# Attention: a batch's layer norm turned by VectorE in blocks of 32 by 32 and sorted by memory, one turn ahead, in place of TensorE transposes

## The chip, the cores and the metric

The kernel runs on one core of a Trainium2 chip. A core has five engines that work side by side, each through its own list of instructions in order: TensorE (PE in the profile; PEld is its weight load), VectorE (DVE), ScalarE (ACT), GpSimd (POOL) and SyncE (SP, which here issues nearly all DMAs). Sixteen DMA engines move data between memory and the core's on-chip memory of 128 partitions (rows); TensorE writes its results to eight banks called PSUM. The metric is the device time of one execution in microseconds.

## What is computed

Three residual blocks over x of 16 batches, 512 tokens and width 256, all in 32-bit floats: half of a feed-forward block (attention over 16 slots and 16 experts), full causal attention with 16 heads, and half of the same feed-forward block again. The change is in the middle one:

```python
x = x + 0.5 * _L0_ffn_ref(_layernorm(x, axis=-1), ...)
x = x + _L0_attn_ref(_layernorm(x, axis=-1), ...)
x = x + 0.5 * _L0_ffn_ref(_layernorm(x, axis=-1), ...)

# _L0_attn_ref: q, k rotated; causal
q = x @ Wq + bq;  kv = x @ Wkv + bkv
scores = jnp.einsum('bqhd,bkhd->bhqk', q, k) * (1.0 / np.sqrt(DQK))
probs = jax.nn.softmax(jnp.where(causal, scores, -jnp.inf), axis=-1)
out = jnp.einsum('bhqk,bkhd->bqhd', probs, v)
return out.transpose(0, 2, 1, 3).reshape(b, s, H * DV) @ Wo + bo
```

The products with Wq and Wk need the layer norm with the width on the partitions, while the layer norm is made with tokens on the partitions. So each batch's layer norm has to be transposed, 512 x 256.

## The kernel before

All of x stays on chip: 16 places `xs[b]`, tokens on the partitions, 4 tiles of 128 tokens by 256.

**Units and turns.** Attention works on 64 units: 16 batches (`b`) times 4 groups (`hg`) of 4 heads. The loop `for u in range(-2, nu)` (L1101) is a pipeline, and one pass of it is called a turn here. Turn u does, for different units: the products of the weights with the values of unit u (`sums`, p_av), the turning of the weights of unit u+1 (`turn_most`, `turn_corner`, `turn_rest`, `move`), scores and exponentials of unit u+2 (p_as), queries and keys of unit u+3 (`queries_keys`, p_q and p_k), values of unit u+1 (p_v), and the output product of unit u (`leave`, p_ay), whose addition to x by VectorE (`added`, kept in `gone`) follows in the next turn.

**Order.** TensorE's order is that of the program throughout. Inside the loop so is that of VectorE, ScalarE, GpSimd and SyncE (`manual_schedule`, L1098). So an instruction waits for all that stand ahead of it on its engine. TensorE's order in a turn: p_av, (p_ahT), p_as of tile 3, p_v, p_q, p_k, p_v, p_as of tiles 2, 1 and 0, p_ay.

**A new batch.** In turn u = 4b + 1 the batch b + 1 comes in (`fresh`, L1105). `enter` (L866) makes its layer norm h on ScalarE from mean and deviation, in two tiles that share their places with two of the rotation's (`rope2`, `rope3`). `with_bias` (L874) adds the output's bias to x on GpSimd. `width` (L878) turns h: 8 TensorE transposes of 128 by 128 into two banks of PSUM (p_ahT, L883), and two ScalarE copies (L884) into `ahT`, of which there are two. In the same turn p_q reads `ahT`. Batch 0 enters before the loop.

**Deviations.** The statistics of tokens (`token_stats`) run ahead by `u + 13`; a pair of batches has its square root on ScalarE (`spread`) in turn u with u + 5 a multiple of 8, and its reciprocal on VectorE (`scales`) one turn later. ScalarE loads another table for the square root and then the one for the exponential again.

**The turning of the weights.** VectorE transposes only within blocks of 32 by 32 (L1001, `STREAM_TRANSPOSE`, into `sq`); 16 DMAs (`move`, L1024, 160 KB each) carry the blocks to their partitions in `prT`, from on-chip memory to on-chip memory. `sq` and `prT` have one buffer each. The slot stage of the feed-forward block does the same through memory: `Squares.turn` (L530), `leave` (L534, one DMA of 512 KB to memory) and `onto` (L538, four DMAs back).

**SyncE** in a turn: the 16 DMAs of `move`, and, in the turn after a batch's last unit (u = 4b), two writes of the result (L1078). The DMAs use eight semaphores in rotation, so a DMA also waits for the one issued eight before it.

Of the kernel before, what the change touches and what calls it, by code (L numbers as in the profile page):

```python
# [9 lines left out]
F32 = mybir.dt.float32  # L10
# [5 lines left out]
P = 128  # L16
NB, S, D = 16, 512, 256
NT = S // P
NC = D // P
GB = 4  # L20
PB = 2
# [14 lines left out]
NHG = AH // HG  # L36
SQ = 32
NSQ = P // SQ
# [9 lines left out]
def macaron_kernel(ctx: ExitStack, tc: tile.TileContext, a: dict, out: bass.AP):  # L48
    nc = tc.nc
# [6 lines left out]
    def ps(name):  # L56
        return psum.tile([P, 512], F32, tag="b", name=name, bufs=8)
# [135 lines left out]
    def token_stats(b, t):  # L193
        g = b // PB
        if b % PB == 0 and t == 0:
            mvs[g] = small.tile([P, PB * NT, 2], F32, tag=f"mv{g}", name=f"mv{g}", bufs=2)
        st = small.tile([P, 6], F32, tag="bnst", name=f"bnst{b}_{t}")
        nc.vector.bn_stats(st, xs[b][:, t, :])
        nc.vector.bn_aggr(mvs[g][:, (b % PB) * NT + t, :], st)
# [17 lines left out]
    def pair_shift(g):  # L217
        shifts[g] = small.tile([P, PB * NT], F32, tag="shift", name=f"shift{g}", bufs=2)
        nc.vector.scalar_tensor_tensor(shifts[g], mvs[g][:, :, 0], -1.0, rstds[g], ALU.mult, ALU.mult)
# [624 lines left out]
    def attention(qp, wq, wk, wv, wo, cos, sin, row):  # L844
# [2 lines left out]
        ap = None  # L847
        units = [(b, hg) for b in range(NB) for hg in range(NHG)]
        nu = len(units)
        hTs, hs, qs, ks, vs, oTs, prTs, stds = {}, {}, {}, {}, {}, {}, {}, {}  # L850

        def spread(g):

            n = PB * NT
            std = small.tile([P, n], F32, tag="std8", name=f"std_g{g}")
            nc.scalar.activation(std, mvs[g][:, :, 1], AF.Sqrt, bias=eps)
            return std

        def scales(g, std):

            n = PB * NT
            rstds[g] = small.tile([P, n], F32, tag=f"rstd{g}", name=f"rstd{g}", bufs=1)
            nc.vector.reciprocal(rstds[g], std)
            pair_shift(g)

        def enter(b):  # L866

            hs[b] = [qp.tile([P, 2, D], F32, tag=f"rope{2 + k}", name=f"h{b}_{k}") for k in range(2)]
            for t in range(NT):
                i = (b % PB) * NT + t  # L870
                nc.scalar.activation(hs[b][t // 2][:, t % 2, :], xs[b][:, t, :], AF.Identity,
                                     bias=shifts[b // PB][:, i:i + 1], scale=rstds[b // PB][:, i:i + 1])

        def with_bias(b):  # L874
            for t in range(NT):
                nc.gpsimd.tensor_tensor(xs[b][:, t, :], xs[b][:, t, :], row, ALU.add)

        def width(b):  # L878
            hTs[b] = qp.tile([P, NC, S], F32, tag="hT", name=f"ahT{b}", bufs=2)
            for c in range(NC):  # L880
                pt = ps(f"p_ahT{b}_{c}")
                for t in range(NT):
                    nc.tensor.transpose(pt[:, t * P:(t + 1) * P], hs[b][t // 2][:, t % 2, c * P:(c + 1) * P], ident)  # L883
                nc.scalar.copy(hTs[b][:, c, :], pt)  # L884

        class Rotated:

# [2 lines left out]
            def __init__(self, u, nm, w, r):  # L890
                self.b, self.hg = units[u]
                self.nm, self.w, self.r, self.m = nm, w, r, {}
# [172 lines left out]
        def leave(u, t0):  # L1065
            b, hg = units[u]
            py = ps(f"p_ay{b}_{hg}_{t0}")
            for t in range(2):
                for pair in range(HG // 2):
                    nc.tensor.matmul(py[:, t * D:(t + 1) * D], oTs[u][:, pair, (t0 + t) * P:(t0 + t + 1) * P],  # L1070
                                     wo[:, hg * (HG // 2) + pair, :],
                                     start=(pair == 0), stop=(pair == HG // 2 - 1))

            def added():
                xt = xs[b][:, t0:t0 + 2, :]
                nc.vector.tensor_tensor(xt, py.rearrange("p (t d) -> p t d", t=2), xt, ALU.add)
                if hg == NHG - 1:
                    nc.sync.dma_start(xout[b][:, t0:t0 + 2, :], xt)  # L1078
            return added
# [4 lines left out]
        def queries_keys(u):  # L1084

            if u >= nu:
                return []
            q = qs[u] = Rotated(u, "q", wq, R_BQ)
            k = ks[u] = Rotated(u, "k", wk, R_BK)
            return [lambda: q.half(0), lambda: (q.half(1), q.add()), lambda: k.half(0), lambda: (k.half(1), k.add())]  # L1090

        scales(0, spread(0))
        enter(0)
        with_bias(0)
        ap = yield [lambda: width(0)] + queries_keys(0)
        ws = {}
        seen = 2 * NHG
        with tc.manual_schedule(engines={mybir.EngineType.DVE, mybir.EngineType.Activation,  # L1098
                                         mybir.EngineType.Pool, mybir.EngineType.SP}):
            gone = []  # L1100
            for u in range(-2, nu):  # L1101
                new = ws[u + 2] = Weights(u + 2) if u + 2 < nu else None
                qk = queries_keys(u + 3)
                old = ws.get(u + 1)
                fresh = u + 3 < nu and units[u + 3][1] == 0  # L1105
                if fresh:
                    enter(units[u + 3][0])
                if u + 2 == nu:
                    old.scaled((1, 0))
                    values(u + 1, 0)  # L1110
                    values(u + 1, 2)
                if u >= 0:
                    sums(u, 0)
                    sums(u, 1)
                if old and u + 2 == nu:
                    old.turn_at_once()
                elif old:
                    old.turn_most(0)
                    old.scaled((1, 0), slice(0, HG // 2))
                    old.turn_most(1)  # L1120
                    old.scaled((1, 0), slice(HG // 2, HG))
                    old.turn_most(2)
                    old.turn_most(3)
                    old.turn_corner()
                    old.turn_rest()
                    old.move()
                for one in gone:
                    one()
                if fresh:
                    with_bias(units[u + 3][0])  # L1130
                if u + 4 in stds:
                    scales((u + 4) // (PB * NHG), stds.pop(u + 4))
                if fresh:
                    width(units[u + 3][0])
                if new:
                    new.scores((3,))
                    new.exps((3,))

                for at in range(seen, min(u + 13, NB * NHG)):
                    token_stats(*divmod(at, NHG))  # L1140
                seen = max(seen, u + 13)
                if u >= NHG + 1:
                    token_stats(*divmod(u - NHG - 1, NHG))
                if new:
                    new.scaled((3,))
                if 0 <= u + 1 < nu - 1:
                    values(u + 1, 0)
                for one in qk:
                    one()
                if 0 <= u + 1 < nu - 1:  # L1150
                    values(u + 1, 2)
                if 0 <= u + 5 < nu and (u + 5) % (PB * NHG) == 0:
                    stds[u + 5] = spread((u + 5) // (PB * NHG))
                if new:
                    new.scores((2,))
                    new.scores((1, 0))
                    new.exps((2,))
                    new.exps((1, 0), lambda: new.scaled((2,)))

                if u == nu - NHG:  # L1160
                    for g in range(NB // PB - 1):
                        pair_rstd(g)
                if u == nu - 1:
                    for g in range(PB):
                        entered[g] = xs[g]
                        for t in range(NT):
                            i = (g % PB) * NT + t
                            nc.vector.tensor_scalar(xs[g][:, t, :], xs[g][:, t, :], mvs[g // PB][:, i, 0:1],
                                                    rstds[g // PB][:, i:i + 1], ALU.subtract, ALU.mult)
                gone = [leave(u, 0), leave(u, 2)] if u >= 0 else []  # L1170
                if u >= nu - 2:
                    for one in gone:
                        one()
                    gone = []
            token_stats(NB - 2, NT - 1)
# [55 lines left out]
```

## Time and profile before

| | us |
|---|---|
| median of 3 runs | 2330.49 (2329.22 to 2330.73) |
| profiled execution, its own time | 2332.58 |
| its span, first to last instruction | 2330.9 |
| mean granted clock of TensorE | 0.993 |

| groups that the change touches (count) | busy us | mean ns of one |
|---|---|---|
| L883 PE MATMUL p_ahT 128x128 (128) | 17.4 | 279 |
| L884 ACT COPY ahT 128x512 (32) | 17.0 | 585 |
| L871 ACT ACTIVATE h 128x256 (64) | 33.1 | 588 |
| L876 POOL TENSOR_TENSOR x 128x256 (64) | 44.7 | 730 |
| L1001 DVE STREAM_TRANSPOSE sq 128x512 (126) | 84.3 | 669 |
| L530 DVE STREAM_TRANSPOSE sqa 128x512 (50) | 34.7 | 708 |
| L898 PE MATMUL p_q 128x512 (512) | 230.5 | 593 |

Durations of TensorE overlap, since matmuls are pipelined: what a group takes is read from the start of it to the start of the next. A line of a timeline has start, length, engine, line, operation, what is written and read, and a count; the time in brackets is idle time before it and what ended it. A line of the table by stretch has, for PE, PEld, DVE, ACT and POOL, busy us and instructions, then TensorE's granted clock, the share of the DMA engines and their GB/s. SyncE's lines stand as SPq: it only issues.

### The profile page before, as it was taken

How to read it: one execution, taken by the hardware profiler on the slowest of the kernel's cores; microseconds unless marked ns; L12 is line 12 of the kernel's file. 1: busy time of each engine (PE TensorE's matmuls, PEld its weight loads, DVE VectorE, ACT ScalarE, POOL GpSimd, SP SyncE). 2: the span in 40 equal slices, each digit the busy share in tenths (PEclk: the TensorE clock that was granted, in tenths of full speed). 3: DMA queues.
4: the chain of work that ended last, by engine and by line, in shares of the span. 5: the costliest groups of instructions: out<-in, count | busy, mean ns of one | idle time of the engine just before them, and what ended most of it. 6: DMA issues, size and time to landing. Idle time of an engine off the chain costs nothing. (4 is left out here: it accounts for less than half of the span.)

```text
span 2330.9 us, 42260 instructions
## 1 busy us (share of the span) xinstructions
PE 2285.0 (98%) x14496; PEld 1453.5 (62%) x14496; DVE 1754.1 (75%) x4658; ACT 1123.7 (48%) x3046; POOL 1061.9 (46%) x1692
## 2 busy tenths in 40 slices
PE   7999999999999999999999999999999999999999
PEld 5665588465656565565656565655656566664588
DVE  6742397888888888898888888888888874442387
ACT  4743243455455545554645545554555454542233
POOL 2210054565555565655656555556565541210043
PEclk9999999999999999999999999999999999999999
DMA  6839851345555464645455555546464543839834
GB/s 223 252 124 406 321 137 46 85 97 129 107 119 126 103 134 93 142 103 129 107 123 113 126 111 116 129 100 137 91 140 105 127 110 96 241 115 405 329 115 140
DMA packets 159710, 346.77 MB, mean 149 GB/s; under 512 B 38980, under 2 KB 98952, under 8 KB 151304
## 3 DMA queue, kind: packets, MB, share of 16 engines
q1 hardware_dynamic: 158636, 343.27, 55.4%
q8 instruction: 115, 1.88, 0.4%
q14 instruction: 99, 0.81, 0.1%
q10 hardware_dynamic: 860, 0.81, 0.1%
HBM read 148.95 MB, written 29.88 MB: 77 GB/s over the span
## 5 line engine op out<-in xcount | busy, mean ns | idle before, releaser
L986 POOL TENSOR_SCALAR pr<-pr,ars 128x512 f32<-128x512 f32 (+3 forms) x1024 | 522.1, 532 | 631.5 <-DVE ars L983 631.5
L978 ACT ACTIVATE pr<-pr,amn 128x512 f32<-128x512 f32 (+3 forms) x1024 | 560.5, 549 | 268.4 <-DVE amn L974 268.2
L974 DVE CUSTOM_DVE_ANT_0 pr<-p_as,causal 128x512 f32<-128x512 f32 (+3 forms) x1024 | 433.9, 484 | 96.6 <-PE p_as L956 96.6
L1001 DVE STREAM_TRANSPOSE sq<-pr 128x768 f32<-128x768 f32 x441 | 379.0, 906 | 0.2 <-issue 0.2
L956 PE MATMUL p_as<-k,q 32*128 32x128 f32 (+3 forms) x4096 | 325.3, 445 | 7.1 <-DVE k L904 3.4
L1054 PE MATMUL p_av<-prT,v 128*64 128x512 f32 (+3 forms) x2048 | 292.1, 438 | 1.9 <-DVE amn L974 1.9
L956 PEld LDWEIGHTS p_as<-k,q 32*128 32x128 f32 x4096 | 192.4, 186 | 107.4 <-issue 49.6
L920 PEld LDWEIGHTS p_v<-wv,ahT 128*128 128x128 f32 x1024 | 189.4, 190 | 97.4 <-issue 75.6
L920 PE MATMUL p_v<-wv,ahT 128*128 128x256 f32 x1024 | 248.1, 385 | 0.0
L923 ACT COPY v<-p_v 128x512 f32<-128x512 f32 x128 | 73.3, 574 | 353.1 <-PE p_v L920 353.1
L1070 PE MATMUL p_ay<-wo,aoT 128*128 128x256 f32 x1024 | 240.5, 388 | 0.2 <-ACT aoT L1061 0.2
L1054 PEld LDWEIGHTS p_av<-prT,v 128*64 128x64 f32 x2048 | 138.1, 138 | 161.7 <-issue 136.5
L898 PE MATMUL p_k<-ahT,wk 128*128 128x512 f32 x512 | 230.6, 592 | 0.4 <-DVE amn L974 0.4
L898 PE MATMUL p_q<-ahT,wq 128*128 128x512 f32 x512 | 230.5, 593 | 0.2 <-ACT ahT L884 0.2
L1070 PEld LDWEIGHTS p_ay<-wo,aoT 128*128 128x128 f32 x1024 | 190.8, 191 | 32.0 <-ACT aoT L1061 0.6
L978 ACT ACTIVATION_READ_ACCUMULATOR pr<-pr,amn 128x1 f32 x1024 | 191.7, 187 | 0.0
L898 PEld LDWEIGHTS p_k<-ahT,wk 128*128 128x128 f32 x512 | 97.2, 190 | 122.7 <-issue 110.5
L898 PEld LDWEIGHTS p_q<-ahT,wq 128*128 128x128 f32 x512 | 97.1, 190 | 95.8 <-issue 85.4
L717 POOL TENSOR_TENSOR kbd<-kT,own 128x256 f32<-128x256 f32 x32 | 19.7, 619 | 267.4 <-DVE kT L680 235.5
L1061 ACT ACTIVATE aoT<-p_av,bcol 128x512 f32<-128x512 f32 x128 | 87.4, 684 | 108.9 <-PE p_av L1054 108.9
L770 PE MATMUL p_cy<-vw,catT 128*128 128x256 f32 x512 | 120.8, 379 | 0.0
L548 PE MATMUL p_ds<-hT,qk 128*128 128x512 f32 x256 | 118.3, 606 | 2.3 <-ACT hT L241 2.3
(167 smaller groups left out, 3252.0 us busy)
## 6 DMA issues: line engine op xcount, KB each, us to landing
prT<-sq SPq DMA_DIRECT2D x1008, 160.0 KB
w<-in_e_W_dram SPq DMA_DIRECT2D x64, 1024.0 KB
w<-in_e_Wg_dram SPq DMA_DIRECT2D x32, 1024.0 KB
out_dram<-x SPq DMA_DIRECT2D x64, 256.0 KB
awaya<-sqa SPq DMA_DIRECT2D x25, 512.0 KB
atT<-awaya SPq DMA_DIRECT2D x100, 128.0 KB
xl<-in_attn_x_dram SPq DMA_DIRECT2D x16, 512.0 KB
xl<-out_dram SPq DMA_DIRECT2D x16, 512.0 KB
```

The source lines that it names most:

```text
L548: nc.tensor.matmul(psc, qk[:, k, c * P:(c + 1) * P], hT[:, k, :], start=(k == 0), stop=(k == NC - 1))
L770: nc.tensor.matmul(py[:, t * D:(t + 1) * D], atT[:, c, t * P:(t + 1) * P], vws[b][:, c, :], start=(c == 0), stop=(c == NC - 1))
L898: nc.tensor.matmul(pq, self.w[:, k, at:at + P], hTs[self.b][:, k, :], start=(k == 0), stop=(k == NC - 1))
L920: nc.tensor.matmul(pv[:, t * 256:(t + 1) * 256], hTs[b][:, k, (t0 + t) * P:(t0 + t + 1) * P], wv[:, k, hg * HG * DQ:(hg + 1) * HG * DQ], s ...
L956: nc.tensor.matmul(banks[j][:, at:at + w], q[n][j * 32:(j + 1) * 32, i * P:(i + 1) * P], k[n][j * 32:(j + 1) * 32, :w], start=(n == 0), st ...
L974: nc.vector.tensor_tensor_reduce(out=self.at(i, j), in0=banks[j][:, at:at + w], in1=causal[:, S - w:], scale=-1.0 / math.sqrt(DQ), scalar= ...
L978: nc.scalar.activation(self.at(i, j), self.at(i, j), AF.Exp, bias=self.mn[:, i, j:j + 1], scale=-1.0, accum_out=self.rs[:, i, j:j + 1])
L986: nc.gpsimd.tensor_scalar(self.at(i, j), self.at(i, j), self.rs[:, i, j:j + 1], 1.0, ALU.mult, ALU.mult)
L1001: nc.vector.transpose(view(self.sq, j * blocks * SQ + dst[0] * SQ, [(blocks * SQ, nh)] + [(s * SQ, n) for s, (_, n) in zip(dst[1:], of)] + ...
L1054: nc.tensor.matmul(po[j * DQ:(j + 1) * DQ, :].rearrange("d (a f) -> d a f", a=NSQ)[:, :, t * SQ:], vs[u][:, t, head * DQ:(head + 1) * DQ], ...
L1061: nc.scalar.activation(oTs[u][:, pair, :].rearrange("d (i a y) -> d a i y", i=NT, a=NSQ), po.rearrange("d (a i y) -> d a i y", i=NT, a=NSQ ...
L1070: nc.tensor.matmul(py[:, t * D:(t + 1) * D], oTs[u][:, pair, (t0 + t) * P:(t0 + t + 1) * P], wo[:, hg * (HG // 2) + pair, :], start=(pair ...
```

## The change

Batches 1 to 15 get their `ahT` in another way, and one turn earlier.

- A batch becomes fresh in turn u = 4b (u + 4 is its first unit) instead of 4b + 1; `enter` and `with_bias` move with it. Statistics, `spread` and `scales` move one turn ahead too.
- In place of `width`, `Trip` lets VectorE transpose the two tiles of h in blocks of 32 by 32 into `ahT`, each block at the place from which one partition group's data are contiguous. `leave` writes the whole `ahT`, 512 KB, to memory. Both stand behind `gone` and `with_bias` and ahead of the scores of tile 3; on SyncE, `leave` stands behind `move` and the result's two writes.
- `land`, at the head of the next turn and ahead of that turn's `move`, reads the blocks back into the same `ahT`: 16 DMAs, one for each pair of partition group k and block row a, each of 32 partitions and 8 pieces of 32 numbers (128 B), 32 KB in all.
- In that same turn p_q reads `ahT`, as before. Batch 0 still goes through `width`.

```diff
+        class Trip:
+            def __init__(self, b):
+                self.b = b
+                hTs[b] = qp.tile([P, NC, S], F32, tag="hT", name=f"ahT{b}", bufs=2)
+                dst = hTs[b].rearrange("p c s -> p (c s)").rearrange("p (k c t x) -> p t c k x", k=NSQ, c=NC, t=NT)
+                for i, h in enumerate(hs[b]):
+                    nc.vector.transpose(dst[:, 2 * i:2 * i + 2],
+                                        h.rearrange("p t (c k y) -> p t c k y", c=NC, k=NSQ))
+            def leave(self):
+                self.mem = away.tile([P, NC * S], F32, tag="away", name=f"away{self.b}")
+                nc.sync.dma_start(self.mem, hTs[self.b].rearrange("p c s -> p (c s)"))
+            def land(self):
+                n = NC * NT
+                for k in range(NSQ):
+                    for a in range(NSQ):
+                        nc.sync.dma_start(
+                            hTs[self.b][k * SQ:(k + 1) * SQ].rearrange("y c s -> y (c s)").rearrange(
+                                "y (n a x) -> a y n x", n=n, a=NSQ)[a],
+                            self.mem[a * SQ:(a + 1) * SQ, k * n * SQ:(k + 1) * n * SQ].rearrange(
+                                "y (n x) -> y n x", n=n))
...
-                fresh = u + 3 < nu and units[u + 3][1] == 0
+                fresh = units[u + 4][0] if 0 < u + 4 < nu and units[u + 4][1] == 0 else None
                 if fresh:
-                    enter(units[u + 3][0])
+                    enter(fresh)
+                if u + 3 in trips:
+                    trips.pop(u + 3).land()
...
                 if fresh:
-                    with_bias(units[u + 3][0])
-                if u + 4 in stds:
-                    scales((u + 4) // (PB * NHG), stds.pop(u + 4))
-                if fresh:
-                    width(units[u + 3][0])
+                    with_bias(fresh)
+                    trips[u + 4] = Trip(fresh)
+                    trips[u + 4].leave()
+                if u + 5 in stds:
+                    scales((u + 5) // (PB * NHG), stds.pop(u + 5))
...
-                for at in range(seen, min(u + 13, NB * NHG)):
+                for at in range(seen, min(u + 14, NB * NHG)):
                     token_stats(*divmod(at, NHG))
-                seen = max(seen, u + 13)
+                seen = max(seen, u + 14)
...
-                if 0 <= u + 5 < nu and (u + 5) % (PB * NHG) == 0:
-                    stds[u + 5] = spread((u + 5) // (PB * NHG))
+                if 0 < u + 6 < nu and (u + 6) % (PB * NHG) == 0:
+                    stds[u + 6] = spread((u + 6) // (PB * NHG))
```

More of the change, by code (lines that the diff above doesn't have):

```diff
@@ L849, in attention @@
         nu = len(units)
-        hTs, hs, qs, ks, vs, oTs, prTs, stds = {}, {}, {}, {}, {}, {}, {}, {}
+        hTs, hs, qs, ks, vs, oTs, prTs, stds, trips = {}, {}, {}, {}, {}, {}, {}, {}, {}
         def spread(g):
@@ L1097, in attention @@
         seen = 2 * NHG
-        with tc.manual_schedule(engines={mybir.EngineType.DVE, mybir.EngineType.Activation,
-                                         mybir.EngineType.Pool, mybir.EngineType.SP}):
+        with tc.tile_pool(name="awayh", bufs=2, space=bass.MemoryType.DRAM) as away, \
+                tc.manual_schedule(engines={mybir.EngineType.DVE, mybir.EngineType.Activation,
+                                            mybir.EngineType.Pool, mybir.EngineType.SP}):
             gone = []
```

## The prediction, made before the change was run

> **What bounds the kernel now.** I read the page's busy table first, then TensorE's timeline over two turns, then SyncE's and the DMA engines' activity in the same stretch. A turn is one pass of the attention loop.
>
> ```profile
> PE 2285.0 (98%) x14496; PEld 1453.5 (62%) x14496; DVE 1754.1 (75%) x4658; ACT 1123.7 (48%) x3046; POOL 1061.9 (46%) x1692
> ```
>
> TensorE is busy for 98% of the span: inside attention a microsecond taken off it, or one in which it waits, moves the end by a microsecond. TensorE's timeline of the turn u = 8 and the beginning of u = 9:
>
> ```profile
> 639.45 4.53 PE L1054 MATMUL p_av<-prT,v 128*64 128x512 f32 x32
> 643.91 2.00 PE L956 MATMUL p_as<-k,q 32*128 32x512 f32 x16
> 645.84 2.00 PE L920 MATMUL p_v<-wv,ahT 128*128 128x256 f32 x8
> 647.67 3.60 PE L898 MATMUL p_q<-ahT,wq 128*128 128x512 f32 x8
> ...
> 662.82 4.53 PE L1054 MATMUL p_av<-prT,v 128*64 128x512 f32 x32
> 667.27 1.09 PE L883 MATMUL p_ahT<-ident,h 128*128 128x128 f32 x8
> 668.30 2.00 PE L956 MATMUL p_as<-k,q 32*128 32x512 f32 x16
> 670.23 1.99 PE L920 MATMUL p_v<-wv,ahT 128*128 128x256 f32 x8
> 672.06 0.59 PE L898 MATMUL p_q<-ahT,wq 128*128 128x512 f32 x1
> ```
>
> No gap stands between the groups. An ordinary turn lasts 662.82 - 639.45 = 23.37 us; one with the eight p_ahT transposes lasts 24.39 (687.21 - 662.82). The difference, 1.02 us, is what the transposes occupy (667.27 to 668.30). The reader should also keep the place of p_q: it is the first reader of a new ahT, 8.22 us into an ordinary turn.
>
> SyncE's timeline and the DMA share in the same turn:
>
> ```profile
> 645.50 10.04 SPq L1024 DMA_DIRECT2D prT<-sq  x16
> 655.66 1.05 SPq L1078 DMA_DIRECT2D out_dram<-x  x2
> 668.88 10.03 SPq L1024 DMA_DIRECT2D prT<-sq  x16
> ```
>
> ```profile
> 655.50:658.50 3.00, 3.00 (x37) 2.12 (x39) 1.36 (x5) 0.58 (x1) 2.65 (x3) 1.00 1.07 210
> 658.50:660.60 2.10, 2.10 (x31) 1.81 (x24) 2.10 (x13) 2.05 (x7) 0.00 (x0) 1.00 0.90 265
> 660.60:662.80 2.20, 2.20 (x11) 1.68 (x9) 2.17 (x14) 2.20 (x11) 1.44 (x3) 1.00 0.03 8
> ```
>
> The last two columns are DMA share and GB/s. SyncE issues from 645.50 to 656.71; the engines are full until 660.6, then idle. Everything that SyncE issues in this turn after the result's two writes lines up behind them. These are not waits today, because nobody needs prT before 662.82.
>
> **What goes.** Fifteen batches (1 to 15; batch 0 keeps TensorE) lose 8 transposes each: 15 x 1.02 = 15.3 us off the bound. The two ACT copies (585 ns each) go too; ACT is busy 11.37 of 23.37 us in this turn, so they are worth nothing.
>
> **What is added on VectorE.** Two 128x512 transposes per batch, in turn 4b after the two residual adds. The groups by shape give 669 ns for this size in attention and 708 ns in the slot stage, and 0.6 us from start to start: 1.2 to 1.4 us. VectorE is busy 20.69 of 23.37 us, so it fits, but the exps of tile 3 come later. How late may they come? Turn u = 12 tells: there ACT's two table loads made VectorE late, exps began at 742.75, 8.81 into the turn instead of 7.08 (646.53), 1.73 late, and TensorE's 48 p_as took 3.51 instead of 2.88, 0.63 lost. So about 1.1 us is free, and the transposes would cost 0.1 to 0.3 in eight of the batches. In the seven batches whose fresh turn follows such a late turn, VectorE is 0.43 early and nothing is lost. These 0.1 to 0.3 are not added below: they push p_q back while the transfer does not move.
>
> **What moves.** enter (ACT, 4 x 588 ns) and with_bias (POOL, 4 x 730 ns) go one turn earlier, into gaps of the same size (POOL stands idle for 7.08 us before its L986 of tile 3). One statistic of a token earlier changes no turn's count but the first's (0.6 us, during the filling of the pipeline). The square root goes a turn earlier, and its 0.63 us stall with it: seven before, seven after.
>
> **What is added on the queue**, and decides. Per batch: one write of 512 KB (leave), issued after move and the two result writes; then 16 reads of 32 KB (land), the first waiting on leave's landing; the next move is queued behind them on SyncE, and p_q waits for the last. On the clock of the turn above, taken as a fresh one:
> - leave is issued at 656.7, behind a full queue. From 660.6 its 128 packets of 4096 B move. The same write in the slot stage (awaya) took 1.3 us from first to last packet, and its semaphore came 0.85 us later; with the 265 GB/s of the row above it is 2.0 us. So it lands at 662.6 to 663.4; I take 662.7.
> - land: 16 issues. The nearest rows are wq and wk, runs of 128 B from memory too, 512 of them in each DMA: 0.55 us from issue to issue; atT<-awaya, 128 runs of 1 KB: 0.47; prT<-sq, the worst: 0.63. land has 256 runs of 128 B. I take 0.52, between the first two; the first step is 0.38, so the last is issued 0.38 + 14 x 0.52 = 7.7 us after the first, at 670.4. By the semaphores of the trace a wq read landed 2.2 us after its issue began: 672.6. A set of 16 issues takes 10.25 us on average where the undisturbed one takes 10.04, so 0.2 for disturbances: 672.8.
> - p_q without the transposes wants to start at 672.06 - 1.02 = 671.04. TensorE waits 1.77 us.
>
> In the fresh turns that follow a late one, move starts 5.62 into the turn (763.55 - 757.93) instead of 6.05: the wait is 0.43 shorter, 1.34. The first fresh turn (u = 0) has no result writes and lasts 25.69 us: no wait. So 7 x 1.77 + 7 x 1.34 = 21.8 us are lost, 15.3 gained: **+6.5 us**.
>
> The next move starts when SyncE is free, about 671 instead of 668.88, and lands 2.2 us later than the 683.5 of today; prT is wanted at 687.21 - 1.02 + 1.77 = 687.96. That is covered, and so is VectorE's next use of sq, by the very wait that p_q makes.
>
> The Trainium skill speaks against the change: "DMA: Bandwidth & Descriptors", section "Rules for kernel authors", says that transfers under 64 KB are mostly overhead, and the section "Anatomy of one DMA" sets about 2.0 us as fixed for each. One after another, 16 of them would be an estimated 33 us, and the wait 25 us more per batch. The wq row has the same fixed part (2.2 us), but its 16 reads overlap and are issued in 9.93 us, so I pay the fixed part once.
>
> **Sum.** The profiled execution took 2332.58 us (span 2330.9); the median of the runs is 2330.49. Added to the median: 2337.
>
> **Rivals.**
> - *The transfer is in time* (the other side). If issues step by 0.41 us or less, the last lands by 671.04 and nothing waits: 2330.5 - 15.3 = 2315. For: small DMAs like brow's were issued in 0.23 us. Against: no back-to-back set with as many runs went under 0.47. At 0.47 the waits are 1.07 and 0.64, in all 12, and the time is 2327; the sign turns at 0.487.
> - *The wait also halves TensorE's clock.* Before the turn u = 0 TensorE stood idle and the granted clock fell: p_av took 6.79 us (447.53 to 454.32) instead of 4.46. A gap of 1.46 us (1904.95 to 1906.41) did not do that, one of 2.24 (1910.15 to 1912.39) did: the clock row from 1913.17 reads 0.50 for 6.83 us. If steps of 0.55 to 0.6 make the waits pass about 2 us, each may cost another 1.7 us (half of 3.41 us, the shortest stretch at 0.50 in the trace's clock records): 14 x 1.7 = 24 on top of 2343, that is 2367.
> - *The 16 reads are made to wait for one another*, since each writes interleaved pieces of the same partitions. Then land takes 16 x 2.2 = 35 us instead of 10: 25 us more for each batch, 2700. Against: DVE and ACT wrote interleaved pieces of prT at once at the end (ACT L1041 began at 1930.38 while DVE L1043 ran to 1930.64).
>
> ```profile
> 1909.75:1913.17 3.42, 1.18 (x9) 0.59 (x11) 1.45 (x7) 3.42 (x10) 0.99 (x2) 1.00 0.85 196
> 1913.17:1920.00 6.83, 6.83 (x37) 5.58 (x33) 3.37 (x22) 5.68 (x24) 4.32 (x8) 0.50 0.87 195
> ```
>
> The skill's "TensorE: Matmul & The Clock Gate", section "What's actually happening", asks for a whole idle window of about 3.4 us before the clock drops; by it no wait of mine would do it. The 2.24 us gap above did, so the row decides, and the rival stays.
>
> **How the numbers follow.** Forecast (steps 0.46 to 0.58, 2326 to 2348): 0.53. In time, or nearly (2315 to 2326): 0.20. Half clock (2350 to 2370): 0.20. Serial reads: 0.04; anything else, slower: 0.03. A measurement of this kernel tells about 0.2% (4.7 us) from no change. Faster (below 2325.8): 0.19, nearly all of "in time". Same (to 2335.2): the forecast's lower part, 0.20. Slower: 0.61. The range cuts about 0.1 at each end: 2319 to 2362; the forecast's own is 2326 to 2348.
>
> **What the profile after would show.** Right: no p_ahT but batch 0's; turns 4b+1 of 23.4 us plus 1.3 to 1.8 us, with TensorE idle just before p_q, released by a DMA of ahT; 16 land issues begin close to the turn's start, in about 8 us; fresh turns 4b within 0.3 of 23.37. Wrong: p_q released without a gap (in time); a granted clock below 1.00 inside attention (half clock); a land set that takes 30 us (serial). What would make me wrong above all is the step of land's issues: 14 of them stand in each wait, and 0.05 us of error is 0.7 us per batch.

## The result and the profile after

The changed kernel takes 2334.28 us (median of 20 runs, 2331.65 to 2335.91), the kernel before 2330.46 (20 runs beside them, 2328.36 to 2334.16). The ratio is 1.0016, with a 95% interval of 1.0009 to 1.0022: slower by 3.8 us, or 0.16%. The forecast was 2337, from 2319 to 2362. The interval excludes a ratio of 1, but by the prediction's own bound of 0.2% (2335.2) the time still counts as the same, to which it gave a chance of 0.20, against 0.61 for slower. The profiled execution took 2335.4 us with a span of 2333.7; both are 2.8 us above those of before.

The new class shifts the line numbers: p_q is L925, p_v L947, p_as L983, p_av L1081, `move` L1051, the result's writes L1105, `leave` L901 and `land` L907. First the page's busy table:

```profile
PE 2275.1 (97%) x14376; PEld 1441.9 (62%) x14376; DVE 1771.4 (76%) x4688; ACT 1109.7 (48%) x3016; POOL 1064.5 (46%) x1692
```

TensorE has 120 matmuls fewer (15 batches of 8) and is busy 9.9 us less, while the span is 2.8 us longer: it now waits where it didn't. VectorE gained 17.3 us of work and ScalarE lost 14.0. TensorE's timeline, for the end of the fresh turn u = 8 and the beginning of u = 9, in which the new `ahT` is first read:

```profile
654.44 2.98 PE L983 MATMUL p_as<-k,q 32*128 32x384 f32 x48
657.36 3.72 PE L1097 MATMUL p_ay<-wo,aoT 128*128 128x256 f32 x16
661.01 4.53 PE L1081 MATMUL p_av<-prT,v 128*64 128x512 f32 x32
665.47 2.00 PE L983 MATMUL p_as<-k,q 32*128 32x512 f32 x16
667.39 1.99 PE L947 MATMUL p_v<-wv,ahT 128*128 128x256 f32 x8
670.47 3.67 PE L925 MATMUL p_q<-ahT,wq 128*128 128x512 f32 x8 [1.08 <-ACT pr L1005]
...
685.69 4.53 PE L1081 MATMUL p_av<-prT,v 128*64 128x512 f32 x32
```

The p_ahT group is gone, and a gap stands ahead of p_q. From one p_av to the next are 24.68 us; an ordinary turn takes 23.37 as before, so this one lost 1.32 (before, it lost 1.02 to the transposes). The bracket shows 1.08 of that; p_q also starts 0.16 later than behind a p_v that it overlaps, and its group takes 3.67 instead of 3.60. SyncE's timeline says what p_q waited for:

```profile
643.60 10.05 SPq L1051 DMA_DIRECT2D prT<-sq  x16
653.77 1.05 SPq L1105 DMA_DIRECT2D out_dram<-x  x2
654.91 0.65 SPq L901 DMA_DIRECT2D away<-ahT  x1
661.15 7.72 SPq L907 DMA_DIRECT2D ahT<-away  x16
668.99 1.15 SPq L1051 DMA_DIRECT2D prT<-sq  x2
```

`leave` is issued at 654.91, and SyncE then stands until 661.15: by the semaphores of the trace the write landed at 661.14, 23.60 us into the fresh turn. Sixteen reads follow, one each 0.49 us; the last is issued at 668.43 and lands at 670.23. p_q starts 0.24 us after that. So the bracket's "ACT pr L1005" is the wrong name. In another batch (u = 41) the same wait carries the right one, and the view of waits has both names, for one and the same thing:

```profile
PE p_q L925 <- ACT pr L1005: 8.8, 10, 1.8
PE p_q L925 <- DMA ahT<-away: 5.8, 4, 2.6
```

The columns are the total in us, the number of times and the longest. That is 14 waits, one for each batch but the first two (batch 0 has no reads; batch 1's last read lands 0.38 us before its p_q starts). The table by stretch, over the end of the fresh turn and the reads, has the DMA share and GB/s at the end:

```profile
655.50:658.50 3.00, 3.00 (x45) 2.63 (x38) 2.76 (x12) 1.86 (x7) 1.98 (x2) 1.00 1.00 252
658.50:660.60 2.10, 2.10 (x11) 1.84 (x11) 2.07 (x16) 2.10 (x10) 1.15 (x3) 1.00 0.70 273
660.60:662.80 2.20, 2.20 (x15) 0.87 (x15) 1.77 (x5) 2.05 (x10) 2.20 (x5) 1.00 0.14 21
662.80:668.90 6.10, 6.10 (x47) 3.42 (x44) 6.10 (x11) 1.50 (x3) 2.13 (x6) 1.00 0.43 67
```

The DMA engines are busy until `leave` has drained behind `prT` and the result, then nearly idle until the first read's data move, and while the reads run they are busy 43% of the time at 67 GB/s. The reads are slow to be issued, not slow to move. The granted clock is 1.00 throughout.

The turns of the whole attention stage add up as follows (from the starts of p_av):

| | us against before |
|---|---|
| transposes of 15 batches gone | -15.4 |
| turns u = 4b + 1 longer than 23.365, 14 batches (0.54 to 2.85) | +18.0 |
| fresh turns u = 8, 16, 24, 32, 40, 48 (0.09 each) and u = 56 (0.38) | +0.9 |
| turn 0 (25.28 instead of 25.69) and turn 61 (29.77 instead of 29.95) | -0.6 |
| sum | +2.9 |

The sum agrees with the span's 2.8.

### The profile page after: what moved, and what is told of

It reads as the page before. It is cut to its first block, busy times and chain, and to the rows that moved or that the text cites. A ratio compares the mean times of both kernels' runs of the same rounds, so it can differ in the third digit from the quotient of the medians.

```text
span 2333.7 us, 42312 instructions
## 1 busy us (share of the span) xinstructions
PE 2275.1 (97%) x14376; PEld 1441.9 (62%) x14376; DVE 1771.4 (76%) x4688; ACT 1109.7 (48%) x3016; POOL 1064.5 (46%) x1692
## 5 line engine op out<-in xcount | busy, mean ns | idle before, releaser
L1005 ACT ACTIVATE pr<-pr,amn 128x512 f32<-128x512 f32 (+3 forms) x1024 | 560.5, 549 | 290.5 <-DVE amn L1001 290.3
L983 PE MATMUL p_as<-k,q 32*128 32x128 f32 (+3 forms) x4096 | 327.6, 446 | 6.6 <-DVE k L931 3.4
L1081 PE MATMUL p_av<-prT,v 128*64 128x512 f32 (+3 forms) x2048 | 291.7, 438 | 1.9 <-DVE amn L1001 1.9
L983 PEld LDWEIGHTS p_as<-k,q 32*128 32x128 f32 x4096 | 194.4, 186 | 107.3 <-issue 44.5
L947 PEld LDWEIGHTS p_v<-wv,ahT 128*128 128x128 f32 x1024 | 189.3, 190 | 97.4 <-issue 73.8
L947 PE MATMUL p_v<-wv,ahT 128*128 128x256 f32 x1024 | 248.1, 385 | 0.0
L925 PE MATMUL p_q<-ahT,wq 128*128 128x512 f32 x512 | 231.6, 595 | 14.9 <-ACT pr L1005 8.8
L1081 PEld LDWEIGHTS p_av<-prT,v 128*64 128x64 f32 x2048 | 137.8, 137 | 161.6 <-issue 136.4
L925 PE MATMUL p_k<-ahT,wk 128*128 128x512 f32 x512 | 230.6, 592 | 0.4 <-DVE amn L1001 0.4
L1005 ACT ACTIVATION_READ_ACCUMULATOR pr<-pr,amn 128x1 f32 x1024 | 191.6, 187 | 0.0
L925 PEld LDWEIGHTS p_k<-ahT,wk 128*128 128x128 f32 x512 | 97.2, 190 | 122.8 <-issue 113.6
L925 PEld LDWEIGHTS p_q<-ahT,wq 128*128 128x128 f32 x512 | 96.0, 190 | 115.0 <-issue 88.0
```

Of the source, the lines that this page charges most:

```text
L925: nc.tensor.matmul(pq, self.w[:, k, at:at + P], hTs[self.b][:, k, :], start=(k == 0), stop=(k == NC - 1))
L947: nc.tensor.matmul(pv[:, t * 256:(t + 1) * 256], hTs[b][:, k, (t0 + t) * P:(t0 + t + 1) * P], wv[:, k, hg * HG * DQ:(hg + 1) * HG * DQ], s ...
L983: nc.tensor.matmul(banks[j][:, at:at + w], q[n][j * 32:(j + 1) * 32, i * P:(i + 1) * P], k[n][j * 32:(j + 1) * 32, :w], start=(n == 0), st ...
L1005: nc.scalar.activation(self.at(i, j), self.at(i, j), AF.Exp, bias=self.mn[:, i, j:j + 1], scale=-1.0, accum_out=self.rs[:, i, j:j + 1])
L1081: nc.tensor.matmul(po[j * DQ:(j + 1) * DQ, :].rearrange("d (a f) -> d a f", a=NSQ)[:, :, t * SQ:], vs[u][:, t, head * DQ:(head + 1) * DQ], ...
```

## The experiments

The theory: the gain is real, and it is lost again to TensorE's wait for the last of the 16 reads, because they can only be issued between `leave`'s landing and p_q. Rivals: VectorE's extra work costs it; or the 16 reads cost by themselves, by their time on SyncE, the late `move` behind them or their 128-byte runs. Each experiment is a difference to the changed kernel. The kernel before, beside the first four, took 2330.3 us (8 runs, 2328.61 to 2330.99), and beside the last two 2330.21 (7 runs).

**1. VectorE's part alone.** The write and the reads are left out, so the blocks stay where VectorE put them.

```diff
-                if u + 3 in trips:
-                    trips.pop(u + 3).land()
+                trips.pop(u + 3, None)
...
-                    trips[u + 4].leave()
```

> The changed kernel without the trip to memory: VectorE's two transposes, enter, with_bias and the earlier statistics stay, the write and the 16 reads are left out, so the blocks of batches 1 to 15 stay unsorted and the output is not the reference's. Theory (p_q waits for the reads, nothing else costs anything): the waits of 18.0 us in the trace of the changed kernel go, 2334.3 - 18.0 = 2316, and turns 4b + 1 last 23.4 us. Rival (VectorE's 15 x 1.2 us = 18 us of transposes delay TensorE): 2331 to 2335, as with the reads. If only the fresh turns' 0.09 us stay of VectorE's part, that is 0.7 us of the 2316.

Measured: 2316.53 us (2315.48 to 2318.28), ratio to before 0.9942 (0.9928 to 0.9957). Every turn 4b + 1 is 23.37 us; the fresh turns u = 8k keep their 0.09. TensorE, in the same turn:

```profile
664.80 2.00 PE L983 MATMUL p_as<-k,q 32*128 32x512 f32 x16
666.73 1.99 PE L947 MATMUL p_v<-wv,ahT 128*128 128x256 f32 x8
668.56 3.60 PE L925 MATMUL p_q<-ahT,wq 128*128 128x512 f32 x8
```

No gap ahead of p_q. So VectorE is not the cause, and the whole trip through memory costs 17.8 us (2334.28 - 2316.53).

**2. `leave` ahead of the result's writes.** The reads' start is brought forward by what the result's two writes take.

```diff
+                if fresh:
+                    trips[u + 4] = Trip(fresh)
+                    trips[u + 4].leave()
                 for one in gone:
                     one()
                 if fresh:
                     with_bias(fresh)
-                    trips[u + 4] = Trip(fresh)
-                    trips[u + 4].leave()
```

> The write of a batch stands ahead of the result's two writes on SyncE (VectorE's transposes ahead of the residual adds). Theory: the write lands 1.75 us earlier (it waited for 512 KB of results: their 1.05 us of issue and some 2 us of transfer), the last read lands about 7.5 instead of 9.2 us into the turn, p_q wants to start at 8.22; of the 18.0 us of waits only those of the disturbed sets stay, about 1.5 us: 2318 (2316 to 2322). Rival (the 16 reads themselves, by contention or by SyncE's time, are what costs): no change, 2333 to 2335.

Measured: 2322.51 us (2321.32 to 2323.79), ratio 0.9966 (0.9953 to 0.9979). The direction is right, the size is not: 7.5 us of waits were left instead of 1.5. SyncE's timeline:

```profile
640.51 10.04 SPq L1051 DMA_DIRECT2D prT<-sq  x16
650.65 0.52 SPq L901 DMA_DIRECT2D away<-ahT  x1
651.28 1.91 SPq L1105 DMA_DIRECT2D out_dram<-x  x2
656.81 8.22 SPq L907 DMA_DIRECT2D ahT<-away  x16
```

`leave` lands 0.7 to 1.7 us earlier, 21.2 to 22.5 us into the fresh turn, but the set of 16 reads takes 8.2 us here instead of 7.72. One of its issues takes 0.94 us where the others take 0.44. Ten of the 14 sets have an issue over 0.6 us, where the changed kernel has one in five; had all of them taken 7.74 us, as the undisturbed do, the last read would have landed ahead of p_q's time in 13 of the 14 batches. The long issues go together with transfers of program code, which the trace lists under the kind "instruction": all 13 issues over 0.6 us here overlapped one, and only 23 of the other 227 did. In the changed kernel it is all 6, and 9 of the other 234. No run moved the code transfers, so that they are the cause is not shown.

In one batch (u = 41) the wait also halved TensorE's clock:

```profile
1421.20 5.37 PE L925 MATMUL p_q<-ahT,wq 128*128 128x512 f32 x8 [1.91 <-DMA ahT<-away]
```

```profile
1421.42:1424.83 3.41, 3.41 (x5) 1.35 (x5) 0.33 (x3) 0.67 (x3) 2.69 (x4) 0.50 0.94 236
```

The second fence is the table by stretch: a granted clock of 0.50 for 3.41 us. p_q took 1.70 us more than the 3.67 of a wait without it, which is the price that the prediction gave to that rival, half clock.

**3. The blocks sorted on the way out.** `leave` becomes four writes that put the blocks in order in memory (runs of 128 B), `land` four reads of whole rows (4 KB on each of 32 partitions).

```diff
-                self.mem = away.tile([P, NC * S], F32, ...)
-                nc.sync.dma_start(self.mem, hTs[self.b].rearrange("p c s -> p (c s)"))
+                self.mem = away.tile([SQ, NSQ * NC * S], F32, ...)
+                for a in range(NSQ):
+                    nc.sync.dma_start(self.mem.rearrange("y (m a x) -> a y m x", a=NSQ, x=SQ)[a], ...)
...
+                for k in range(NSQ):
+                    nc.sync.dma_start(hTs[self.b][k * SQ:(k + 1) * SQ].rearrange("y c s -> y (c s)"),
+                                      self.mem[:, k * NC * S:(k + 1) * NC * S])
```

> The blocks are sorted by the write instead of by the reads: four writes of 128 KB in runs of 128 B, four reads of 128 KB in runs of 4 KB; 8 DMAs instead of 17, 4 instead of 16 of them behind the landing of the write. Theory (what counts is the number of DMAs that are issued after the write has landed, 0.49 us each): the writes take SyncE 1.5 us more and the DMA engines 2 to 4 us more, the reads 1.8 instead of 7.7 us; the last read lands 4 to 6 us into the turn, no wait: 2317 (2315 to 2320). Rival (runs of 128 B are slow wherever they stand): the writes to memory take 6 us longer than now and the waits stay, 2331 to 2340.

Measured: 2316.71 us (2315.96 to 2317.09), ratio 0.9942 (0.9925 to 0.9959): as fast as the kernel without any trip, and faster than both kernels. SyncE's timeline, and TensorE's:

```profile
642.66 9.47 SPq L1050 DMA_DIRECT2D prT<-sq  x15
652.25 1.05 SPq L1104 DMA_DIRECT2D out_dram<-x  x2
653.40 6.70 SPq L903 DMA_DIRECT2D away<-ahT  x4
662.26 1.73 SPq L909 DMA_DIRECT2D ahT<-away  x4
665.48 5.01 SPq L1050 DMA_DIRECT2D prT<-sq  x8
```

```profile
665.88 1.99 PE L946 MATMUL p_v<-wv,ahT 128*128 128x256 f32 x8
667.71 3.60 PE L924 MATMUL p_q<-ahT,wq 128*128 128x512 f32 x8
```

The four writes take SyncE 6.70 us behind full DMA engines, and the last lands 26.14 us into the fresh turn, 2.5 later than the single write. But SyncE has nothing else to do then. The reads need 4.1 us from first issue to last landing (662.26 to 666.40) instead of 9.1 (661.15 to 670.23), and in all batches the last lands at least 1.3 us ahead of p_q. The runs of 128 B are as many as before; what changed is on which side of the fixed moment they stand, and how many issues come after it.

**4. Twice as many reads.** Each read is cut into two, 16 KB each, with the same bytes and runs.

```diff
-                        nc.sync.dma_start(... [a], ...)
+                        for i in range(2):
+                            nc.sync.dma_start(... [a][:, i * m:(i + 1) * m], ...)
```

> Each read is cut in two: 32 reads of 16 KB instead of 16 of 32 KB, the same bytes and the same runs. Theory (0.45 to 0.49 us of SyncE's time for each issue): 7.2 to 7.9 us more for each of 15 batches, 108 to 118 us: 2442 to 2453, turns 4b + 1 of 31.5 to 33 us with TensorE idle for 8 to 9 us ahead of p_q. If such gaps halve TensorE's clock, 1.7 to 3.4 us more per batch: 2468 to 2504 and a granted clock of 0.5 in these turns. Rival (the bytes and runs count, not the number of DMAs): 2334 to 2340.

Measured, one execution: 2469.23 us. The reads are issued every 0.47 us, hardly less than the 0.49 of reads twice as large:

```profile
675.37 0.63 SPq L901 DMA_DIRECT2D away<-ahT  x1
681.59 15.05 SPq L909 DMA_DIRECT2D ahT<-away  x32
```

```profile
697.67 5.31 PE L927 MATMUL p_q<-ahT,wq 128*128 128x512 f32 x8 [7.81 <-DMA ahT<-away]
```

With the same bytes and runs in all, the set takes 7.3 us more: the count of the DMAs sets the wait, not their bytes. The turns 4b + 1 are longer by 8.7 to 11.4 us, 152 in all, and part of that is the clock: in each of the 15 gaps (6.93 to 8.82 us) it falls to 0.50, for 6.83 or 10.24 us, as in two batches of the table by stretch:

```profile
485.93:492.76 6.83, 4.23 (x5) 1.85 (x6) 0.44 (x1) 0.00 (x0) 1.09 (x2) 0.50 0.64 149
588.33:598.57 10.24, 4.99 (x6) 2.19 (x7) 1.20 (x2) 0.00 (x0) 2.03 (x4) 0.50 0.58 129
```

**5. Two turns ahead.** The same 1 + 16 DMAs, but a whole turn between `land` and p_q, and `leave` in a turn without the result's writes.

```diff
-                fresh = units[u + 4][0] if 0 < u + 4 < nu and units[u + 4][1] == 0 else None
+                fresh = units[u + 5][0] if 0 < u + 5 < nu and units[u + 5][1] == 0 else None
...
-                if u + 3 in trips:
-                    trips.pop(u + 3).land()
+                if u + 4 in trips:
+                    trips.pop(u + 4).land()
```

The statistics, `spread` and `scales` move one more turn in the same way.

> The changed kernel with the fresh batch taken two turns ahead instead of one (enter, with_bias, Trip and leave at turn 4b-1, land at turn 4b; the same 1 + 16 DMAs a batch). The fresh turn now has no result writes ahead of leave, and p_q reads ahT a whole turn after land. Theory (the loss is TensorE's wait for the last of the 16 reads, because leave's landing leaves only 8.2 us to them): no wait ahead of p_q, turns 4b+1 of 23.4 us; the 18.0 us of waits go, 2334.3 - 18.0 = 2316, and no more than 2318.5 if VectorE's transposes meet the square root's turns. Rival (the loss is the 16 reads themselves: their time on SyncE, the late move of prT behind them, or their traffic): that stays, 2322 or more, and the lost time shows in turn 4b or 4b+1 as a wait for prT, for VectorE or for sq.

Measured: 2316.44 us (2315.98 to 2317.54), ratio 0.9941 (0.9924 to 0.9957). SyncE, and TensorE in the turn that reads `ahT`:

```profile
627.80 0.52 SPq L901 DMA_DIRECT2D away<-ahT  x1
633.21 9.09 SPq L907 DMA_DIRECT2D ahT<-away  x16
642.41 10.04 SPq L1051 DMA_DIRECT2D prT<-sq  x16
```

```profile
664.82 1.99 PE L947 MATMUL p_v<-wv,ahT 128*128 128x256 f32 x8
666.65 3.60 PE L925 MATMUL p_q<-ahT,wq 128*128 128x512 f32 x8
```

This set of reads even took 9.09 us and pushed `move` to 642.41, and nothing waited for either. So the reads' time on SyncE and the late `move` cost nothing by themselves.

**6. The reads without the write.** They take other data, which have long been in memory.

```diff
+                mem = a_in["attn_x"][self.b].rearrange("(p t) d -> p (t d)", p=P)
...
-                            self.mem[a * SQ:(a + 1) * SQ, ...
+                            mem[a * SQ:(a + 1) * SQ, ...
...
-                    trips[u + 4].leave()
```

> The changed kernel without leave: the 16 reads of land take the batch's rows of attn_x from memory instead of what leave wrote (the same runs of 128 B, count and place in the program; ahT then holds numbers that are not the layer norm's, so the result isn't the reference's). Theory (the reads are late only because the first of them waits for leave's landing at 23.6 us into the fresh turn): the first read is issued right after the result's two writes, about 17.3 us into the fresh turn, the last lands some 9.5 us later, about 3.5 us into the next turn, ahead of p_q at 8.2: no wait, turns 4b+1 of 23.4 us, 2316 (to 2318.5). Rival (16 reads of 128-byte runs cost by themselves, wherever they lie): turns 4b or 4b+1 stay 0.5 us or more longer, 2322 or more. It also prices the step of the reads' issues when the DMA engines still carry prT and the result: 0.49 us if the issue alone sets it, more if the full engines do.

Measured: 2317.0 us (2316.27 to 2317.42), ratio 0.9941 (0.9926 to 0.9956).

```profile
651.60 1.05 SPq L1108 DMA_DIRECT2D out_dram<-x  x2
652.74 10.40 SPq L910 DMA_DIRECT2D ahT<-in_attn_x_dram  x16
```

```profile
665.25 1.99 PE L950 MATMUL p_v<-wv,ahT 128*128 128x256 f32 x8
667.08 3.60 PE L928 MATMUL p_q<-ahT,wq 128*128 128x512 f32 x8
```

The reads begin right behind the result's writes; the last lands at 664.58, 2.5 us before p_q wants it. The set is longer here (10.40 us: its issues step by 0.53 to 1.34 us until 659.24 and by 0.49 from then on; the DMA engines are full until about 657), and still costs nothing. With 5 this settles it: neither the reads nor their runs of 128 B cost time, only their beginning at a moment that leaves some 8 us for 9.1.

## Why the prediction was right, step by step

It named the bound and the mechanism, and 2337 was 2.7 us too high. The sign was right too, but by little, and partly by luck, as said below. By its own steps:

- *15 x 1.02 us gained.* Right: 15.4 by the turns of before, and experiment 1, which has nothing but this and VectorE's part, gains 13.8 us of the time.
- *VectorE's transposes cost 0.1 to 0.3 us in eight of the batches, absorbed by the wait.* Six fresh turns are 0.09 longer and u = 56 is 0.38 longer, 0.9 in all. Since p_q is wanted that much later while `leave` lands when it did, this is a part of the forecast's 21.8 and not an addition, as the step said. Where nothing waits it is paid openly: experiment 1 keeps the 0.09.
- *`leave` lands 23.25 us into the fresh turn, 22.82 in those that follow a late one.* Measured on average 23.3 and 22.9; single batches lie between 22.45 and 23.61.
- *16 issues at 0.52 us, 7.7 from first to last, and 0.2 for disturbances.* The step was 0.49, so 7.28 undisturbed; the disturbed sets bring the mean to 7.62. That is 0.28 less than the 7.9 of the sum.
- *The last read lands 2.2 us after its issue.* This is the term that was most mis-sized: 1.85 on average, 0.35 less. The row that it came from, wq, has twice as many runs and bytes in each DMA; that this is the reason was not tested.
- *p_q starts with the landing.* It starts 0.28 us after it on average (0.09 to 0.46), and a restart costs some 0.07 more, as the p_q of 3.67 us shows. This was not counted, and takes back 0.35 of those 0.63.
- *The sign.* By the prediction's own sum it turns at a step of 0.487 us, and the undisturbed step was 0.49. That the 0.35 of the landing and the 0.35 of the start cancel is luck: had p_q started with the landing, as the sum has it, the 14 waits would be an estimated 4.9 us shorter (14 x 0.35), and the trace's +2.8 would be -2.1. The long issues, for which the sum had 0.2 us a batch, weigh as much: 14 x (7.62 - 7.28) = 4.8 us.
- *Waits of 1.77 and 1.34 us, 21.8 in all.* Measured 1.51 and 1.06 on average, 18.0 in all, and 18.9 with the 0.9 of the fresh turns; none for batch 1, as forecast, though not for the lack of the result's writes: its write landed 23.06 us into the turn, like the others', and the turn of 25.28 us left room. So this was 2.9 us too high (0.2 to 0.3 for each batch, as the terms above give), and turns 0 and 61 gave another 0.6 that was not forecast: +2.9 by the trace where the sum had +6.5. The medians differ by 3.8; the 0.9 between that and the trace is less than the spread of single runs.
- *The next `move` is covered.* Right: in u = 9 `prT` landed at 683.50, and the products that read it start at 685.69.
- *The stall of the square root moves by a turn.* Right: 0.63 us, seven before, in u = 8k + 4, and seven after, in u = 8k + 3.

The rivals: *in time* fell: the step was 0.49 and not 0.41 us. An earlier write (2), fewer reads behind it (3) or an earlier turn (5) takes part of the wait away or all of it. *Half clock* did not come in the profiled execution of the changed kernel, whose longest gap was 2.6 us; its price was right where it came (experiment 2). *Serial reads* fell: 16 reads that write pieces of the same partitions are issued every 0.49 us, and one lands 1.9 us after its issue (the median of all 240). The Trainium skill's fixed 2.0 us of each DMA ("DMA: Bandwidth & Descriptors", section "Anatomy of one DMA") is given there for DMAs that GpSimd issues; these, which SyncE issues, come near it. The landing is paid once for a set and not 16 times, as the 9.1 us from first issue to last landing show.

## What to carry to other kernels

Where data go through memory with a deadline, count the DMAs that can only be issued after the write has landed: here each cost SyncE 0.49 us at 32 KB and 0.47 at 16 KB, and the small runs belong on the side that has time, which was the write. A transfer that is a little late is made harmless either by fewer issues behind the landing (4 reads, 4.1 us) or by one more turn of lead; both gave the full 14 us here (ratios 0.9942 and 0.9941). And 16 reads of small runs are not dear in themselves; the same reads cost nothing or 18 us by when they may start.

## What was not expected of the hardware

Whether a gap halves TensorE's clock is not told by its length. In the changed kernel, at u = 41, TensorE stood for 2.6 us ahead of p_q and kept the full clock, while 1.91 us in experiment 2 halved it. The table by stretch of the changed kernel:

```profile
1430.00:1432.60 2.60, 0.02 (x1) 0.00 (x1) 2.35 (x9) 2.60 (x9) 0.00 (x0) 1.00 0.57 102
1432.60:1436.40 3.80, 3.77 (x9) 1.81 (x10) 1.47 (x3) 0.22 (x1) 2.70 (x4) 1.00 0.91 228
```

Within one trace all clock records begin at multiples of 3.413 us from one another, so a gap can lie within one such stretch or across two. That does not explain it either: the stretch before the drop in experiment 2 (1418.01 to 1421.42) was 44% busy, and the one with the gap here (1430.64 to 1434.05) 42%, without a drop. What decides stays open. The Trainium skill ("TensorE: Matmul & The Clock Gate", section "What's actually happening") asks for a whole idle window of about 3.4 us; the gap of 1.91 us differs from that, and the 15 gaps of 6.93 us and more in experiment 4, each with a fall to half the clock, agree.

A set of 16 DMAs whose data lie on 128-byte runs is now and then held up by a long issue, of 0.63 to 1.94 us where the others take 0.45: six of 240 in the changed kernel, 13 with `leave` moved ahead and 7 in experiment 5. Each of these 26 overlapped a transfer of program code; of the 694 other issues of these three traces, 38 did. The longest, in the batch of u = 41, by SyncE's timeline, and the code transfer in the DMA view of 1424.8 to 1426.7:

```profile
1424.78 1.94 SPq L907 DMA_DIRECT2D ahT<-away  x1
```

```profile
q8 instruction: 1, 0.02, 4.5%
```

The three longest waits of the changed kernel (u = 41, 21 and 49) each have such an issue. Whether the code transfers cause them was not tested, and most of the issues beside one in experiment 2 (23 of 36) were not long.
